# A modulated recurrence and a top-2 expert layer on one core: another first stage, and the last blocks' loads in branches

## The chip, the cores and the metric

The kernel runs on one core of a Trainium2 chip. A core has five engines with an instruction queue each: TensorE (PE in the profile, with its weight loads as PEld), VectorE (DVE), ScalarE (ACT), GpSimd (POOL) and SyncE (SP), and DMA engines that move data between the memory and the core. SP only starts DMAs here. The engines wait for one another and for DMAs through semaphores, each in the order of its own queue. The metric is the time of one execution on the device in microseconds (us). The median of three runs before is 823.8.

## The reference

The input x has 4 batches of 1024 tokens with 256 numbers each. A small product gives six rows per batch (shift, scale and gate for each of two layers). The first layer is a gated linear recurrence, the second a mixture of 8 experts of which each token uses two.

```python
mod = (_silu(L0_c) @ L0_wmod).reshape(L0_c.shape[0], 6, 1, -1)
sa, ca, ga, sb, cb, gb = (mod[:, 0], mod[:, 1], mod[:, 2], mod[:, 3], mod[:, 4], mod[:, 5])
h = _layernorm(x, axis=-1) * (1 + ca) + sa
x = x + ga * _L0_attn_ref(h, ...)
h = _layernorm(x, axis=-1) * (1 + cb) + sb
x = x + gb * _L0_ffn_ref(h, ...)
# first layer, on the rms-normalized h (256 -> 512 -> 256)
K = sigmoid(xn @ W_K)
u, g_in, g_out = split(xn @ W_ugg, 3)
u = u * sigmoid(g_in) * (1.0 - K)
outputs = scan along the tokens: s[t] = K[t-1] * s[t-1] + u[t]
y = (outputs * sigmoid(g_out)) @ W_out + residual
# second layer: softmax over 8 experts, the best two, rescaled to sum 1
output += (gelu(x @ W1[e] + b1[e]) @ W2[e] + b2[e]) * combine_w[e]
```

The two gates ga and gb have their size raised to at least 0.25 with the sign kept. All is in 32-bit floats.

## The kernel before

**Order.** The order of the work on each engine is written out by hand: instructions enter the queues as the program issues them, and no scheduler moves them. Waits are put in by the framework from what each instruction reads and writes.

**First stage.** SP loads c, then wmod in two pieces (the first 512 columns, then the other 1024), wk, the three parts of wu, x of chunk 1, wo and x of chunk 2; ACT's queue loads x of chunk 0. `sc` is c times its sigmoid; PE turns it (L251) into `scT` (4 columns) and DVE spreads batch 0 over 128 columns (`scB`). With scB, `first_rows` (L272) makes the first five modulation rows of batch 0, already spread over all partitions, in three products pm, pm1 and pm2. DVE makes `mda` (shift and 1 + scale) from pm; ACT copies pm1 and pm2 into `mdf`, between the four squares of chunk 0. With scT, `all_rows` (L286) makes the six rows for all four batches; they are finished in `other_rows` and stored to a small `rows` buffer in memory, from which later batches load their copies.

**First layer.** The 4096 tokens are 8 chunks of 512 tokens, two to a batch. For a chunk, `a_stats` and `shift` compute the statistics (a power on POOL), `a_norm` normalizes on ACT in four tiles of 128 tokens, `a_mod` applies scale and shift on DVE over the whole chunk (L365, L366), `a_square` sums squares on ACT, `a_root` and `a_scale` scale (with a power on POOL), and `a_turn` transposes on PE; ACT copies the two halves to `hT`. `project(c, hc)` runs four times per chunk: four products (pk, pgi, pu, pgo; L429) in four PSUM banks, the sigmoids on ACT, the recurrence as a scan on DVE. While chunk c is projected, the next chunk is prepared in calls between the products. `a_skip` (the residual) and `scale_out` (the gate folded into W_out) come early in a batch's first chunk. The gate row gb of a batch is loaded by SP (`load_gb`) and stored next to each token's row by ACT's queue (`store_gb`, L337).

**Second layer.** Each token's two choices go into lists per expert, and the lists are cut into blocks of 256 tokens of one expert (128 in a half block). A block j needs its list entries (`ent`, loaded by SP), its rows (two gathers by POOL, `fetch_rows`, L801) and its expert's weights (`fetch_weights`, SP, L819 to L822; 1 MB each for w1 and w2). `work` does a first product with gelu (`b_up`, L859), transposes the next block's rows (`b_turn`, L843) and a second product (`b_down`, L889); DVE adds the bias and multiplies with the weights, and POOL adds the rows to the output in memory (`add_rows`, L876). In the last blocks the rows of the last part are kept in `last_y`, with their places in `last_at`, and added at the start of the next block.

**Last blocks.** How many blocks there are depends on the data: at least 32 and at most 39. From block 28 on, `work_either` chooses between a whole and a half block (L1074); from block 32 on `rest` is a nest of branches on the number of blocks (L1105), each inside the one before. At the start of block j, `fetch(j)` starts the rows of j + 2 and the weights of j + 1, whether these blocks exist or not. A branch is taken by all five engines, each on its own copy of the number.

Of the kernel before, what the change touches and what calls it, by code (L numbers as in the profile page):

```python
# [9 lines left out]
F32 = mybir.dt.float32  # L10
I32 = mybir.dt.int32
AF = mybir.ActivationFunctionType
ALU = mybir.AluOpType
# [6 lines left out]
def tile_adaln_block(  # L20
# [33 lines left out]
    P = 128  # L54
# [191 lines left out]
    nc.scalar.activation(sc, c_sb, AF.Sigmoid)  # L246
    nc.vector.tensor_mul(sc, sc, c_sb)
    scT = setup.tile([P, KC, B], F32, tag="scT", name="scT")
    pt = ps_tr.tile([P, TB], F32, tag="tr", name="pt_c")
    for k in range(KC):  # L250
        nc.tensor.transpose(pt[:, k * B : (k + 1) * B], sc[:, ts(k, P)], ident[:B, :B])  # L251
# [1 line left out]

    scB = setup.tile([P, KC, P], F32, tag="scB", name="scB")
    nc.vector.tensor_copy(scB, scT[:, :, 0:1].broadcast_to((P, KC, P)))
    mda = deep.tile([P, 2, D], F32, tag="mda", name="mda_0")
    mdf = deep.tile([P, 3, D], F32, tag="mdf", name="mdf_0")
    with nc.allow_non_contiguous_dma(reason="a few hundred elements, once"):
        nc.scalar.dma_start(out=rms_sb, in_=rms_scale.rearrange("(k p) -> p k", p=P))
        nc.scalar.dma_start(out=split_sb, in_=split_scale.rearrange("(k p) -> p k", p=P))  # L260
# [3 lines left out]
    X[0]["stats"] = stats(X[0]["x"], "a0")  # L264
    shift(0)
    a_norm(0)

    def first_rows(i: int):
        w = min(TB, 5 * D - i * TB)
        pm = ps_mm.tile([P, TB], F32, tag="mm", name=f"pm0_{i}")  # L270
        for k in range(KC):
            nc.tensor.matmul(  # L272
                pm[:, :w],
                lhsT=scB[:, k, :],
                rhs=wmod_sb[:, k, ds(i * TB, w)],
                start=(k == 0),
                stop=(k == KC - 1),
            )
        return pm

    rows_sb = setup.tile([B, 6, D], F32, tag="rows_sb", name="rows_sb")

    def all_rows(i: int):
        pm = ps_mm.tile([P, TB], F32, tag="mm", name=f"pm_{i}")
        for k in range(KC):
            nc.tensor.matmul(  # L286
                pm[:B, :],
                lhsT=scT[:, k, :],
                rhs=wmod_sb[:, k, ts(i, TB)],
                start=(k == 0),  # L290
                stop=(k == KC - 1),
            )
        nc.scalar.copy(rows_sb[:, 2 * i : 2 * i + 2, :].rearrange("b r d -> b (r d)"), pm[:B, :])

    pm = first_rows(0)
    nc.vector.tensor_scalar_add(mda[:, 1, :], pm[:, D:], 1.0)
    nc.scalar.copy(mda[:, 0, :], pm[:, :D])
    pm1, pm2 = first_rows(1), first_rows(2)

    def other_rows():  # L300
        for j in (1, 4):
            nc.vector.tensor_scalar_add(rows_sb[:, j, :], rows_sb[:, j, :], 1.0)
        for j in (2, 5):
            clamp_gate(rows_sb[:, j, :], f"r{j}")
        nc.sync.dma_start(out=rows, in_=rows_sb)
        b1T = setup.tile([P, E, FC], F32, tag="b1T", name="b1T")
        pb = ps_tr.tile([P, TB], F32, tag="tr", name="pt_b1")
        nc.tensor.transpose(pb[:, : E * FC], b1_sb, ident[: E * FC, : E * FC])
        nc.vector.tensor_copy(b1T.rearrange("p e c -> p (e c)"), pb[:, : E * FC])
        nc.sync.dma_start(out=lists.rearrange("(p r) c -> p r c", p=P), in_=pre)  # L310
        with nc.allow_non_contiguous_dma(reason="rows of 32 bytes, once"):
            nc.sync.dma_start(out=b1d.rearrange("e p c -> p e c"), in_=b1T)


    MDA, MDF = {0: mda}, {0: mdf}

    def load_mda(b: int):
        if b < B:
# [15 lines left out]

    def store_gb(b: int):
        hx_gates.append(
            nc.scalar.dma_start(  # L337
                out=hx[ts(b, S), D:].rearrange("(n p) d -> p n d", p=P),
                in_=GB[b].unsqueeze(1).broadcast_to((P, NT, D)),
            )  # L340
        )

    def wide_row(row):
        return row.unsqueeze(1).broadcast_to((P, TPB, D))
# [10 lines left out]
    def a_stats(c_):  # L355
        X[c_]["stats"] = stats(X[c_]["x"], f"a{c_}")

    def a_mod(c_, by_tile: bool = False):
        h, md = X[c_]["h"], MDA[c_ // NB]
        if by_tile:  # L360
            for n in range(TPB):
                nc.vector.tensor_mul(h[:, n, :], h[:, n, :], md[:, 1, :])
                nc.vector.tensor_add(h[:, n, :], h[:, n, :], md[:, 0, :])
        else:
            nc.vector.tensor_mul(h, h, wide_row(md[:, 1, :]))  # L365
            nc.vector.tensor_add(h, h, wide_row(md[:, 0, :]))  # L366

    def a_square(c_, also=()):
        u = work.tile([P, TPB, D], F32, tag="u", name=f"u_{c_}", bufs=1)
        X[c_]["u"] = u  # L370
        h = X[c_]["h"]
        ss = small.tile([P, TPB], F32, tag="ss", name=f"ss_{c_}")
        X[c_]["ss"] = ss
        for n in range(TPB):
            nc.scalar.activation(
                u[:, n, :], h[:, n, :], AF.Square, accum_out=ss[:, n : n + 1]
            )
            if n < len(also):
                also[n]()

    def a_root(c_):
        ss = X[c_]["ss"]
        nc.vector.tensor_scalar(ss, ss, 1.0 / D, 1e-30, ALU.mult, ALU.max)
        nc.gpsimd.tensor_tensor(ss, ss, expo[:, 1, :], ALU.pow)

    def a_scale(c_):
        h, ss, u = X[c_]["h"], X[c_]["ss"], X[c_]["u"]
        nc.vector.tensor_scalar_add(ss, ss, RMS_EPS)
        nc.vector.reciprocal(ss, ss)
        for n in range(TPB):  # L390
            nc.vector.tensor_scalar_mul(u[:, n, :], h[:, n, :], ss[:, n : n + 1])
# [433 lines left out]
    def fetch(j: int):  # L825

        fetch_rows(j + 2)
        fetch_weights(j + 1)

    def wait_for(ins, others):  # L830
        for other in others:
            tc.add_manual_dep(
                ins.ins, other.ins.name,
                mybir.DependencyInfo(mybir.DependencyClass.Sync, mybir.DependencyReason.DATA),
                reason="all of it is there",
            )
# [46 lines left out]
    def b_down(j: int, half: bool = False, mid=None, keep: bool = False):  # L883

        g, w2, b2b, ent, hb = (BK[j][n] for n in ("g", "w2", "b2b", "ent", "hb"))
        for t in range(1 if half else HK):
            py = ps_y.tile([P, D], F32, tag="y", name=f"pye_{j}_{t}_{half}")
            for fc in range(FC):
                nc.tensor.matmul(  # L889
                    py,  # L890
                    lhsT=g[:, fc, ts(t, P)],
                    rhs=w2[:, fc, :],
                    start=(fc == 0),
                    stop=(fc == FC - 1),
                )
            kept_back = keep and t == (0 if half else HK - 1)
            if kept_back:
                yb, at = last_y, last_at
            else:
                yb = xpool.tile([P, D], F32, tag="yb", name=f"yb_{j}_{t}_{half}", bufs=3)  # L900
                at = ent[:, t, 0:1]
            nc.vector.tensor_add(yb, py, b2b)  # L902
            nc.vector.scalar_tensor_tensor(  # L903
                yb, yb, ent[:, t, 1:2].bitcast(F32), hb[t][:, D:], ALU.mult, ALU.mult
            )
            if kept_back:
                nc.vector.tensor_copy(last_at, ent[:, t, 0:1])
                continue
            if t > 0:
                nc.gpsimd.memset(between, 0.0)  # L910
            ins = add_rows(yb, at, seen(j))
            for other in BK[j]["acc"]:
                tc.declare_no_dep(ins.ins, other.ins, reason="a block's tokens are distinct")
            BK[j]["acc"].append(ins)
            if t == 0 and mid is not None:
                mid()


    a_mod(0)
    a_square(  # L920
        0,
        [
            lambda: nc.scalar.copy(mdf[:, 0:2, :].rearrange("p r d -> p (r d)"), pm1),
            lambda: nc.scalar.activation(
                mdf[:, 2, :], pm2[:, :D], AF.Identity, bias=ones[:, 0:1]
            ),
        ],
    )
    a_root(0)
    nc.vector.tensor_mul(rs_sb, rms_sb, split_sb)  # L930
    for i in range(6 * D // TB):
        all_rows(i)
    a_scale(0)
    a_turn(0)
    clamp_gate(mdf[:, 0, :], "0")
    a_stats(1)
    for c_ in range(NCH):
        nxt, prv, old = c_ + 1, c_ - 1, c_ - 2
# [12 lines left out]
        drain(6)  # L951
        if more:
            a_mod(nxt)
        a_skip(c_)
        if was:
            o_pe(prv)
            o_resid(prv)
        if placed is not None:
# [4 lines left out]
            load_mdf(b + 1)  # L963


        if part == 0:
            scale_out(b)
        if was:
            f_stats(prv)
        project(c_, 1, [lambda: a_square(nxt)] if more else [])  # L970
        if c_ == 0:
            other_rows()
        drain(6)
        if placed is not None:
            r_rank_pe(placed)
# [41 lines left out]
            a_stats(c_ + 2)  # L1017


        if was:  # L1020
            f_mod(prv)
            f_store(prv)
# [75 lines left out]
        ends_at[0:1, 1:2], min_val=sure, max_val=NJ, skip_runtime_bounds_check_because=why  # L1098
    )
    for j in range(sure_whole, sure):  # L1100
        fetch(j)
        work_either(j, j == sure - 1)

    def rest(j: int):
        with tc.If(n_blocks > j):  # L1105
            add_rows(last_y, last_at, T)
            fetch(j)
            work_either(j, True)
            if j + 1 < NJ:
                rest(j + 1)  # L1110
# [37 lines left out]
```

## Time and profile before

| what | us |
|---|---|
| median of three runs (lowest, highest) | 823.8 (823.59, 825.05) |
| the profiled execution's own time | 824.49 |
| its span, from the first to the last instruction | 822.8 |
| TensorE busy | 800.3 |
| first projection product starts | 19.78 |
| last matmul ends | 809.99 |
| last scatter to the output starts | 813.97 |

All times in the profile count from the first instruction of the profiled execution. A row of a group or of the timeline gives start, duration, engine, line and operation, written as out<-in, and in brackets the idle time before it and what ended it. In the chain of waits each piece is what the end of the execution depended on, followed backwards. A queue's own instructions (DMA starts, branches) have a q behind the engine's name. [...] each product of 256 rows deep weights (two halves of 128) shows as four matmuls.

### The profile page before, as it was taken

To read this page: it belongs to the slowest core of one execution; us is meant where nothing else is said; L and a number is where in the kernel's file an instruction comes from. 1 tells how busy PE (TensorE), PEld (TensorE's weight loads), DVE (VectorE), ACT (ScalarE), POOL (GpSimd) and SP (SyncE) were. 2 spreads that over 40 slices of the span, in tenths; PEclk is the share of its full clock that TensorE was granted. 3 is DMA by queue.
4 is the path that set the end of the run, shared out by engine and by line. 5 is a ranking of instruction groups with operands and counts; after the bars stand their busy time and mean duration, and the time that the engine had idled before them with its cause. 6 is when DMAs were issued, how large, how long until landed. Compare 5 with 4: busy or idle time off the path is not lost.

```text
span 822.8 us, 10559 instructions
## 1 busy us (share of the span) xinstructions
PE 800.3 (97%) x3447; PEld 604.8 (74%) x3447; DVE 349.3 (42%) x811; ACT 250.7 (30%) x577; POOL 300.7 (37%) x378
## 2 busy tenths in 40 slices
PE   6999999999999999999999999999999999999983
PEld 2454656564656558888888888888888888888973
DVE  4887776797788846554211112111111112111211
ACT  4434243534253243222222221312222221312221
POOL 2003010108302830788742433434342433434432
PEclk9999999999999999999999999999999999999998
DMA  9041222114101265598787677868677777867693
GB/s 305 4 113 45 81 91 72 46 51 78 45 27 33 78 187 160 146 252 206 187 258 233 180 213 209 232 199 225 192 222 200 217 217 208 231 192 199 178 329 105
DMA packets 110048, 132.57 MB, mean 161 GB/s; under 512 B 25686, under 2 KB 93978, under 8 KB 109984
## 3 DMA queue, kind: packets, MB, share of 16 engines
q1 hardware_dynamic: 86480, 101.76, 40.3%
q0 software_dynamic: 17776, 25.25, 13.7%
q10 hardware_dynamic: 5728, 4.77, 2.2%
q8 instruction: 33, 0.54, 0.3%
q14 instruction: 31, 0.25, 0.1%
HBM read 113.53 MB, written 21.75 MB: 164 GB/s over the span
## 4 chain that ended last, share of the span: by engine, by line
PE 83%; DMA 7%; DVE 4%; issue 3%; POOL 1%; ACT 1%; POOLq 0%; SPq 0%; another core or an unknown queue 0%; DVEq 0%
PE ph_False L859 24%; PE pye_False L889 23%; PE pya L466 7%; PE pk L429 6%; PE pu L429 6%; PE pgi L429 6%; PE pgo L429 6%; DMA out_dram<-yb_False,ent 3%; DMA out_dram<-last_y,last_at 2%; PE pl L540 2%; PE ptx L843 2%; DMA hb<-hx,ent 1%; PE ptf L403 1%; DMA ent<-lists 1%; PE pta L403 1%
## 5 line engine op out<-in xcount | busy, mean ns | idle before, releaser
L889 PE MATMUL pye_False<-w,g_False 128*128 128x256 f32 x992 | 219.4, 379 | 0.0
L859 PE MATMUL ph_False<-xT,w 128*128 128x256 f32 x992 | 219.2, 379 | 0.0
L859 PEld LDWEIGHTS ph_False<-xT,w 128*128 128x128 f32 x992 | 188.3, 190 | 25.5
L889 PEld LDWEIGHTS pye_False<-w,g_False 128*128 128x128 f32 x992 | 186.1, 190 | 24.0
L868 ACT ACTIVATE g_False<-ph_False,bb 128x256 f32<-128x256 f32 x248 | 104.1, 471 | 313.1 <-issue 225.3
L876 POOL DMA_INDIRECT out_dram<-yb_False,ent x46 | 73.8, 1604 | 188.6 <-DVE yb_False L903 188.6
L845 DVE COPY xT<-ptx 128x512 f32<-128x512 f32 x37 | 25.6, 691 | 197.0 <-PE ptx L843 197.0
L902 DVE TENSOR_TENSOR yb_False<-pye_False,b2b 128x256 f32<-128x256 f32 x62 | 26.3, 424 | 154.8 <-PE pye_False L889 154.8
L559 POOL DMA_INDIRECT lists<-pay,placei x64 | 68.2, 1066 | 12.5 <-issue 11.5
L801 POOL DMA_INDIRECT hb<-hx,ent x60 | 63.0, 1050 | 23.5 <-issue 16.2
L429 PE MATMUL pk<-hT,wk_sb 128*128 128x512 f32 x128 | 61.0, 599 | 0.8 <-ACT hT L405 0.8
L429 PE MATMUL pu<-hT,wu_sb 128*128 128x512 f32 x128 | 60.2, 592 | 0.0
L429 PE MATMUL pgo<-hT,wu_sb 128*128 128x512 f32 x128 | 60.1, 592 | 0.0
L429 PE MATMUL pgi<-hT,wu_sb 128*128 128x512 f32 x128 | 60.1, 592 | 0.0
L466 PE MATMUL pya<-wo,z 128*128 128x256 f32 x256 | 56.6, 379 | 0.0
L214 POOL TENSOR_TENSOR rstd_f<-rstd_f,expo 128x4 f32<-128x4 f32 x8 | 8.2, 1019 | 131.5 <-DVE rstd_f L213 131.5
L466 PEld LDWEIGHTS pya<-wo,z 128*128 128x128 f32 x256 | 48.6, 190 | 9.5 <-issue 3.3
L429 PEld LDWEIGHTS pgi<-hT,wu_sb 128*128 128x128 f32 x128 | 24.3, 190 | 30.6 <-issue 30.6
L429 PEld LDWEIGHTS pgo<-hT,wu_sb 128*128 128x128 f32 x128 | 24.3, 190 | 30.6 <-issue 26.5
L429 PEld LDWEIGHTS pu<-hT,wu_sb 128*128 128x128 f32 x128 | 23.7, 190 | 26.8 <-issue 24.4
L429 PEld LDWEIGHTS pk<-hT,wk_sb 128*128 128x128 f32 x128 | 23.1, 190 | 24.9 <-issue 20.5
L446 DVE TENSOR_TENSOR nu<-nu,pu 128x512 f32<-128x512 f32 x32 | 22.0, 686 | 45.5 <-PE pu L429 33.8
(189 smaller groups left out, 754.4 us busy)
## 6 DMA issues: line engine op xcount, KB each, us to landing
w<-in_L_ffn_W_dram SPq DMA_DIRECT2D x74, 1024.0 KB, 6.4
b2b<-in_L_ffn_b_dram SPq DMA_DIRECT2D x37, 128.0 KB, 6.7
hx<-gb ACTq DMA_DIRECT2D x4, 1024.0 KB, 7.1
out_dram<-x SPq DMA_DIRECT2D x8, 512.0 KB, 3.4
hx<-h SPq DMA_DIRECT2D x8, 512.0 KB, 3.4
x<-in_L_attn_x_dram SPq DMA_DIRECT2D x7, 512.0 KB, 7.2
wu_sb<-in_L_attn_W_ugg_dram SPq DMA_DIRECT2D x3, 512.0 KB, 5.2
mdf<-rows SPq DMA_DIRECT2D x3, 384.0 KB, 4.4
```

Source lines behind the costliest of these rows:

```text
L403: nc.tensor.transpose(pt[:, ts(t, P)], src[:, t, ts(k, P)], ident)
L429: nc.tensor.matmul(ps, lhsT=w[:, k, col : col + P], rhs=hT[:, k, :], start=(k == 0), stop=(k == KC - 1),)
L446: nc.vector.tensor_mul(nu, nu, product(wu_sb, hc * P, "u"))
L466: nc.tensor.matmul(py[:, t, :], lhsT=z[hc][:, ts(2 * q + t, P)], rhs=wo[:, hc, :], start=(hc == 0), stop=(hc == HC - 1),)
L559: ins = nc.gpsimd.indirect_dma_start(out=lists[:, :], out_offset=IndirectOffsetOnAxis(ap=place, axis=0), in_=what, in_offset=None, bounds_ ...
L801: nc.gpsimd.indirect_dma_start(out=g, out_offset=None, in_=hx[: seen(j), :], in_offset=IndirectOffsetOnAxis(ap=BK[j]["ent"][:, t, 0:1], ax ...
L845: nc.vector.tensor_copy(xT, pt)
L859: nc.tensor.matmul(ph[:, u, :], lhsT=w1[:, k, ts(fc, P)], rhs=xT[:, k, :n], start=(k == 0), stop=(k == KC - 1),)
L868: nc.scalar.activation(g[:, fc, :n], ph[:, u, :], AF.Gelu_apprx_tanh, bias=bb[:, fc : fc + 1])
L876: return nc.gpsimd.indirect_dma_start(out=out_rows[:n], out_offset=IndirectOffsetOnAxis(ap=at, axis=0), in_=yb, in_offset=None, bounds_che ...
L889: nc.tensor.matmul(py, lhsT=g[:, fc, ts(t, P)], rhs=w2[:, fc, :], start=(fc == 0), stop=(fc == FC - 1),)
L902: nc.vector.tensor_add(yb, py, b2b)
```

## The change

In the first stage `first_rows` with pm1 and pm2 is gone. Only pm is made for batch 0, later in program order; the two modulation operations take it straight from PSUM, tile by tile; `mda` is filled behind the squares, and mdf for batch 0 is loaded from the `rows` buffer like that of the other batches. `keep_busy(n)` issues n transposes of the constant identity into an unused bank, at three places. The turn of chunk 0 goes tile by tile, and DVE copies its second half to hT. `other_rows` moves up ahead of chunk 1's statistics, `a_skip` and `scale_out` of chunk 0 move back behind chunk 2's, and the gate's store goes from ACT's queue to SP's. In the last blocks `fetch_used` puts the loads that belong to blocks from 32 on into branches of their own. `last_at` is copied ahead of the last rows instead of behind them.

```diff
+    idle = ps_y.tile([P, TB], F32, tag="y", name="idle")
+    def keep_busy(n: int):
+        for _ in range(n):
+            nc.tensor.transpose(idle[:, :P], ident, ident)
+    keep_busy(14)
     pt = ps_tr.tile([P, TB], F32, tag="tr", name="pt_c")
...
     nc.vector.tensor_copy(scB, scT[:, :, 0:1].broadcast_to((P, KC, P)))
+    keep_busy(8)
...
-    pm = first_rows(0)
-    nc.vector.tensor_scalar_add(mda[:, 1, :], pm[:, D:], 1.0)
-    nc.scalar.copy(mda[:, 0, :], pm[:, :D])
-    pm1, pm2 = first_rows(1), first_rows(2)
...
-            nc.scalar.dma_start(
+            nc.sync.dma_start(
                 out=hx[ts(b, S), D:].rearrange("(n p) d -> p n d", p=P),
...
+    def fetch_used(j: int):
+        def used(i: int, step):
+            if i < sure:
+                step(i)
+            elif i < NJ:
+                with tc.If(n_blocks > i):
+                    step(i)
+        used(j + 2, fetch_rows)
+        used(j + 1, fetch_weights)
...
             if kept_back:
                 yb, at = last_y, last_at
+                nc.vector.tensor_copy(last_at, ent[:, t, 0:1])
...
-    a_mod(0)
-    a_square(
-        0,
-        [
-            lambda: nc.scalar.copy(mdf[:, 0:2, :].rearrange("p r d -> p (r d)"), pm1),
-            lambda: nc.scalar.activation(
-                mdf[:, 2, :], pm2[:, :D], AF.Identity, bias=ones[:, 0:1]
-            ),
-        ],
-    )
+    pm = ps_mm.tile([P, TB], F32, tag="mm", name="pm0")
+    for k in range(KC):
+        nc.tensor.matmul(
+            pm, lhsT=scB[:, k, :], rhs=wmod_sb[:, k, :TB], start=(k == 0), stop=(k == KC - 1)
+        )
+    h = X[0]["h"]
+    for n in range(TPB):
+        nc.vector.scalar_tensor_tensor(
+            h[:, n, :], pm[:, D:], 1.0, h[:, n, :], ALU.add, ALU.mult
+        )
+        nc.vector.tensor_add(h[:, n, :], h[:, n, :], pm[:, :D])
+    a_square(0)
+    nc.scalar.copy(mda[:, 0, :], pm[:, :D])
     a_root(0)
+    nc.vector.tensor_scalar_add(mda[:, 1, :], pm[:, D:], 1.0)
     nc.vector.tensor_mul(rs_sb, rms_sb, split_sb)
     for i in range(6 * D // TB):
         all_rows(i)
+    keep_busy(18)
     a_scale(0)
-    a_turn(0)
-    clamp_gate(mdf[:, 0, :], "0")
+    pts = [ps_tr.tile([P, TB], F32, tag="tr", name=f"pta0_{k}") for k in range(KC)]
+    for t in range(TPB):
+        for k in range(KC):
+            nc.tensor.transpose(pts[k][:, ts(t, P)], X[0]["u"][:, t, ts(k, P)], ident)
+    nc.scalar.activation(hT[:, 0, :], pts[0], AF.Copy, scale=rs_sb[:, 0:1])
+    nc.vector.tensor_scalar_mul(hT[:, 1, :], pts[1], rs_sb[:, 1:2])
+    other_rows()
+    load_mdf(0)
     a_stats(1)
...
-        a_skip(c_)
         if was:
+            a_skip(c_)
...
-        if part == 0:
+        if part == 0 and was:
             scale_out(b)
...
         if c_ == 0:
-            other_rows()
+            first_contents()
...
+        if not was:
+            a_skip(c_)
+            scale_out(b)
...
-        fetch(j)
+        fetch_used(j)
         work_either(j, j == sure - 1)
...
         with tc.If(n_blocks > j):
             add_rows(last_y, last_at, T)
-            fetch(j)
+            fetch_used(j)
             work_either(j, True)
```

More of the change, by code (lines that the diff above doesn't have):

```diff
@@ L255, in tile_adaln_block @@
     nc.vector.tensor_copy(scB, scT[:, :, 0:1].broadcast_to((P, KC, P)))
+    keep_busy(8)
     mda = deep.tile([P, 2, D], F32, tag="mda", name="mda_0")
-    mdf = deep.tile([P, 3, D], F32, tag="mdf", name="mdf_0")
     with nc.allow_non_contiguous_dma(reason="a few hundred elements, once"):
@@ L266, in tile_adaln_block @@
     a_norm(0)
[L268 to L277, printed above, removed]
-            )
-        return pm
     rows_sb = setup.tile([B, 6, D], F32, tag="rows_sb", name="rows_sb")
@@ L305, in other_rows, with first_contents @@
         nc.sync.dma_start(out=rows, in_=rows_sb)
+    def first_contents():
         b1T = setup.tile([P, E, FC], F32, tag="b1T", name="b1T")
@@ L312, in other_rows @@
             nc.sync.dma_start(out=b1d.rearrange("e p c -> p e c"), in_=b1T)
-    MDA, MDF = {0: mda}, {0: mdf}
+    MDA, MDF = {0: mda}, {}
     def load_mda(b: int):
@@ L356, in a_stats, with a_mod, a_square @@
         X[c_]["stats"] = stats(X[c_]["x"], f"a{c_}")
-    def a_mod(c_, by_tile: bool = False):
+    def a_mod(c_):
         h, md = X[c_]["h"], MDA[c_ // NB]
[L360 to L368, printed above, removed]
+        nc.vector.tensor_mul(h, h, wide_row(md[:, 1, :]))
+        nc.vector.tensor_add(h, h, wide_row(md[:, 0, :]))
+    def a_square(c_):
         u = work.tile([P, TPB, D], F32, tag="u", name=f"u_{c_}", bufs=1)
@@ L377, in a_square @@
             )
-            if n < len(also):
-                also[n]()
     def a_root(c_):
@@ L906, in b_down @@
             if kept_back:
-                nc.vector.tensor_copy(last_at, ent[:, t, 0:1])
                 continue
@@ L916, in b_down @@
                 mid()
-    a_mod(0)
-    a_square(
-        0,
-        [
-            lambda: nc.scalar.copy(mdf[:, 0:2, :].rearrange("p r d -> p (r d)"), pm1),
-            lambda: nc.scalar.activation(
-                mdf[:, 2, :], pm2[:, :D], AF.Identity, bias=ones[:, 0:1]
-            ),
-        ],
-    )
+    pm = ps_mm.tile([P, TB], F32, tag="mm", name="pm0")
[11 more added lines that the diff above has]
+    nc.scalar.copy(mda[:, 0, :], pm[:, :D])
     a_root(0)
+    nc.vector.tensor_scalar_add(mda[:, 1, :], pm[:, D:], 1.0)
     nc.vector.tensor_mul(rs_sb, rms_sb, split_sb)
@@ L932, in tile_adaln_block @@
         all_rows(i)
+    keep_busy(18)
     a_scale(0)
-    a_turn(0)
-    clamp_gate(mdf[:, 0, :], "0")
+    hT = deep.tile([P, KC, TB], F32, tag="hT", name="hT_0")
+    X[0]["hT"] = hT
+    pts = [ps_tr.tile([P, TB], F32, tag="tr", name=f"pta0_{k}") for k in range(KC)]
[6 more added lines that the diff above has]
+    load_mdf(0)
     a_stats(1)
```

## The prediction

> **What bounds the kernel now.** I read the shares first, then the windows, then the chain of waits at both ends, because a core that is busy 97% of the time has its idle time in few places.
>
> ```profile
> span 822.8 us, 10559 instructions
> PE 800.3 (97%) x3447; PEld 604.8 (74%) x3447; DVE 349.3 (42%) x811; ACT 250.7 (30%) x577; POOL 300.7 (37%) x378
> ```
>
> TensorE (PE) is idle for 22.5 us. The windows (PE busy time is the third number) say where:
>
> ```profile
> 19.80:49.20 29.40, 28.99 (x74) 12.93 (x74) 23.92 (x55) 11.51 (x30) 2.01 (x2) 1.00 0.19 39
> 49.20:776.00 726.80, 726.56 (x3132) 558.77 (x3133) 309.10 (x711) 221.00 (x495) 277.22 (x315) 1.00 0.57 159
> 776.00:810.00 34.00, 31.36 (x210) 28.10 (x208) 6.66 (x16) 9.15 (x32) 14.59 (x12) 1.00 0.90 287
> 810.00:822.80 12.80, 0.00 (x0) 0.00 (x0) 0.97 (x3) 0.00 (x0) 1.62 (x1) 0.71 0.06 7
> ```
>
> From 49 to 776 us PE loses 0.24 us: nothing that the change does to other engines there can show. What counts is when the first projection starts (19.78), a hiccup at 49.20, and what follows the last matmul (810.0). The chain of the beginning (start, duration, what):
>
> ```profile
> 1.26 4.89 DMA wmod_sb<-in_L_wmod_dram
> 6.29 3.68 PE pm L272 x4
> 10.00 0.43 DVE mda L296
> 10.53 1.24 DVE h L365
> 11.86 1.24 DVE h L366
> ...
> 13.62 0.47 ACT mdf L923
> ...
> 15.69 0.03 DVE ss L383
> ...
> 19.78 1.98 PE pk L429 x4
> ```
>
> Four matmul halves of 512 columns take 3.68 us here; the next groups of four take 1.72. The array runs at half rate until 9.80: matmul starts are 0.85 apart before it, 0.43 after. Then two whole-width operations, then squares with two copies for mdf (0.47 and 0.36) between them. The hiccup, in time order:
>
> ```profile
> 46.99 0.38 ACTq L337 DMA_DIRECT2D hx<-gb  x1
> 47.42 0.60 ACT L439 ACTIVATE kt<-pk 128x512 f32<-128x512 f32 x1 [5.68 <-PE pu L429]
> 49.20 1.55 PE L429 MATMUL pk<-hT,wk_sb 128*128 128x512 f32 x3 [0.41 <-ACT hT L405]
> ```
>
> ScalarE (ACT) stands 5.7 us before the store of the gate, because that store waits for gb (issued 44.06, landed 46.97), and the copy of hT for chunk 1 is behind it. The end, POOL's operations:
>
> ```profile
> 803.75 1.61 POOL L876 DMA_INDIRECT out_dram<-last_y,last_at  x1 [3.52 <-DMA ent<-lists]
> 805.66 1.04 POOL L801 DMA_INDIRECT hb<-hx,ent  x1 [0.30 <-issue]
> 807.01 1.00 POOL L801 DMA_INDIRECT hb<-hx,ent  x1 [0.31 <-PE pye_True L889]
> 813.97 1.62 POOL L876 DMA_INDIRECT out_dram<-last_y,last_at  x1 [5.97 <-issue]
> ```
>
> DVE has the last rows ready at 811.96, but their scatter starts at 813.97: POOL is held in the exit of the nested branches (the chain of waits comes to it from the gather of 805.66). 37 weight loads were issued, so the last block is number 35 and the gathers at 805.66 and 807.01 are for block 37, which doesn't exist. The trace's events say that POOL waits there for the scatter of 803.75 (landed 810.76) and that gather (811.06), and then raises a DMA counter until 812.72, an operation which is on the page of the branch line too:
>
> ```profile
> L1074 POOLq INC_SWDGE_SEM  x5: 1361/1448/1568, 771.8 to 805.0; - x5
> ```
>
> **The change, part by part.** *New first stage.* 14 turns of the constant now stand ahead of pt_c. The constant is ready at 1.37 (POOL's select, 1.08 + 0.29); a cold turn of 128 columns is a quarter of 0.85, 0.21 (0.233 if the warm pitch of 0.1166 in the half blocks is doubled), so they end at 1.45 + 3.0 to 3.3 = 4.4 to 4.7, and pt_c comes at about 4.6, not 3.59. Behind it on DVE wait scT, scB and then the statistics of x, which began at 4.93 (x landed at 4.90). scB's end moves from 4.46 to 5.2 to 5.6: the statistics are 0.4 to 0.7 late, I take 0.55. So the first normalized tile, 8.26 + 0.52 before, is there at about 9.4. The new product pm starts when wmod is there (6.15, unchanged; the 8 further turns end before) at 6.3 and takes 1.72 + 0.26 if the array is fast: 8.3. So h decides, not pm, with 1.1 us to spare. The modulation is 8 operations of 128x256 out of PSUM; the nearest rows (L902, L903) follow each other by 0.40 to 0.46: 3.4 to 3.7, I take 3.6, end 13.0. The last tile's square and readout take 0.51 (15.16 to 15.67 before), so the root's operation starts at 13.6 instead of 15.69: **-2.1**. Everything to pk (pow 1.02, scaling, turns, hT) follows at the same distance: pk at 17.7. On PE, pm, 12 matmul halves for all rows (12 x 0.43) and 18 turns (18 x 0.11) end at 8.0 + 5.2 + 2.0 = 15.2, before the first scaled tile (15.7). The copy of the second half of hT on DVE beside ACT's takes away the small stall of the first pk (1.98 against 1.72; half of it start-up): **-0.1**.
>
> [...] The row: half rate until 3.5 us of continuous matmuls had passed (6.29 to 9.80). [...] all turns here are transposes, and no stretch of this trace has only turns. By the row alone the array is fast by about 5 to 8 us and pm costs nothing. [...] I take the row, since real matmuls and turns use the same array[...].
>
> *Moved work.* other_rows (ten DVE operations, 37.99 to 41.11, so 3.1) goes ahead of the statistics of chunk 1: their normalization on ACT comes about 6.9 us after pk, not 4.2. PE needs the bank that ACT frees behind it (go of part 0) 12.0 after pk, and gets it at 9.5: hidden with 2.5 to spare. a_skip and scale_out (3 x 1.22) go behind the statistics of chunk 2, ahead of the last part's nu: that frees its bank at about pk + 28.6, needed at pk + 31.8. If these covers were gone, PE would wait one for one. SP issues the rows' store 20 us sooner, then mdf(0), and load 3 of x moves behind both (from 13.05 to about 24; its statistics run near 65). The gate's store is now on SP, where the next things behind it (x, hx) are wanted tens of us later, and ACT is free: the 0.41 at 49.20 and the slow start after it go, **-0.5**.
>
> *The end.* Three loads fall away: rows 36, rows 37, weights 36 (0.5 + 0.5 + 2.1 MB). None was wanted by PE, but they ran at 0.86 of all DMA engines from 802 to 810. The scatter of 803.75 took 7.0 us to land among them; the last one, alone, took 3.8 (813.97 to 817.77). After: it lands at about 807.6 to 808.5 on the old time scale, DVE needn't wait for it (810.95 becomes 810.0), the rows are ready at 811.0 and the scatter can go at 811.2. POOL now raises a counter for the skipped gather (1.45), for the half block (1.45) and at the exit (1.5): 804.5 to 808.0, then to about 810.1, and 1.25 to the scatter as before (812.72 to 813.97): 811.4. So POOL and DVE meet, and it starts at 811.4 or so instead of 813.97: **-2.5**. last_at's copy only changes sides. If the scatter still takes 7.0 to land, POOL is free at 813.6 and the part is worth 0.3.
>
> *What the branches cost.* Two more branches for each of blocks 31 to 35, one in 30, on every engine. Compare-and-branch has 0.05 us on ACT, SP, DVE and POOL and 0.18 on PE in this trace; PE's for block 35 ran at 798.7, 3.5 us ahead of the work. Hidden, except some 0.2 on SP per block while DMA is full (0.99 and 1.05 of the engines from 783 to 802). I put **+0.3**; bounds 0 and 1.5.
>
> Sum: -2.1 - 0.1 - 0.5 - 2.5 + 0.3 = -4.9 against the profiled execution's span of 822.8 (its own time is 824.5, the median of the runs 823.8; the difference lies outside the parts that change). Predicted: 823.8 - 4.9 = **818.9**.
>
> **Rivals.** (1) *The turns don't warm the array*: first stage -0.8, sum -3.6, 820.2. [...] against it nothing that this trace can show. (2) *The end stays*: the scatter lands late anyway or the three counter raises hold POOL; then -2.6, 821.2. For it: each raise is 1.4 to 1.6. (3) *Loads in line, slower*: in the built program a completion semaphore is reused after four loads in the branches, not eight; the load bb of the next block waits for w2 of this one, and w2 for b2b. On the old scale w2 of block 34 is issued at 790.1 (b2b landed 789.84), not 783.8, and needed at 798.8; that of 35 at 797.2, needed at 806.4. Rooms of 8.7 and 9.2 us, and landings in this stretch are 4.8 / 6.9 / 11.8 (least, median, most). At 11.8 each PE waits 3.1 + 2.6 = 5.7: 824.6, slower. It decides from (8.7 + 9.2 + 4.9) / 2 = 11.4 us per load. Against it: less is then in flight. (4) *A cover is gone in chunk 0*, PE waits 2 us for a bank: 820.9.
>
> **How the numbers follow.** 0.50 for the forecast (its own range 817.8 to 820.0), 0.23 for rival 1, 0.13 for rival 2, 0.05 for rival 3, 0.09 for rival 4 and lesser slips. Below 817.6 a gain would be needed that no step above holds; about 1 in 10 is left on either side of 817.6 to 821.6. A measurement of this kernel tells 0.2% (1.65 us) from no change: faster (below 822.15) takes the forecast, rival 1, nearly all of 2 and most of 4, 0.89; same 0.06; slower 0.05.
>
> **What would show it.** pk first at about 17.7; pm's four halves in 1.7 (row)[...]; no hx store on ACT and no wait at the second chunk's pk; three weight and row loads fewer; the last scatter 1.4 us or so after the last matmul instead of 4. Wrong if pk stays above 19, if PE waits in the half blocks grow beyond today's 2.6 us (the windows: 34.00 less 31.36), or if the exit still holds POOL.

## The result

The changed kernel takes 817.2 us (median of 8 runs) beside 823.7 for the kernel before: ratio 0.9926, 95% interval 0.9905 to 0.9946. Timed again beside other runs of the kernel before it took 817.6 where that one took 824.4, ratio 0.9919 (0.9900 to 0.9938). The prediction was 818.9, which is 0.9941 of 823.8: the direction and most parts held, and the gain (6.5 and 6.9 us) is 1.6 to 2.0 us larger than the sum of 4.9. The first median lies 0.4 below the range that was given (817.6 to 821.6), the second at its lower end.

The profiled execution of the changed kernel took 816.9. The first rows of its page, and its windows with the same bounds of stages as before (first projection, second chunk's first projection, late blocks, what follows the last matmul). A window's row gives its bounds and length, then busy time and count of PE, PEld, DVE, ACT and POOL, then granted clock, DMA share and GB/s:

```profile
span 815.1 us, 10691 instructions
PE 800.9 (98%) x3479; PEld 608.3 (75%) x3479; DVE 350.1 (43%) x814; ACT 249.9 (31%) x574; POOL 299.1 (37%) x374
```

```profile
17.30:46.14 28.84, 28.84 (x73) 13.14 (x74) 24.49 (x56) 11.66 (x29) 3.93 (x3) 1.00 0.45 133
46.14:770.00 723.86, 723.62 (x3120) 556.16 (x3119) 308.43 (x710) 220.67 (x493) 276.75 (x313) 1.00 0.56 157
770.00:805.30 35.30, 33.42 (x223) 30.66 (x221) 7.55 (x18) 9.64 (x34) 11.55 (x9) 1.00 0.77 234
805.30:815.10 9.80, 0.00 (x0) 0.00 (x0) 0.91 (x2) 0.00 (x0) 1.55 (x1) 0.77 0.09 11
```

TensorE is busy 0.6 us longer and idle 14.2 us instead of 22.5. The idle time shrank in three places: before the first projection, ahead of the second chunk's, and at the end. (A fourth, the half blocks, differs from one execution to the next; see below.) The chain of waits at the beginning:

```profile
1.43 3.25 PE idle L254 x14
4.68 0.32 PE pt_c L259 x2
...
5.51 0.67 DVE st_a L210 x2
6.18 1.94 PE pm L920 x4
8.12 5.24 PE pm L281 x12
13.36 2.12 PE idle L254 x18
15.48 1.05 PE pta L943 x7
16.53 0.02 issue
16.55 0.70 ACT hT L944
17.25 0.04 issue
17.30 1.98 PE pk L414 x4
```

The product pm now takes 1.94 instead of 3.68, and PE is busy almost without a pause from 1.43 to 16.5. The first projection starts at 17.30, not 19.78. The window 17.30 to 46.14 has no idle time at all: the hiccup ahead of the second chunk's projection (then 0.41) is gone. At the end, POOL's two scatters and what DVE does between them:

```profile
799.10 1.58 POOL L874 DMA_INDIRECT out_dram<-last_y,last_at  x1 [7.63 <-DVE last_y L902]
802.95 0.15 DVE L897 COPY last_at<-ent 128x1 int32<-128x1 int32 x1 [0.30 <-DMA out_dram<-last_y,last_at]
805.79 0.48 DVE L902 SCALAR_TENSOR_TENSOR last_y<-last_y,ent,hb 128x256 f32<-128x256 f32 x1
806.61 1.55 POOL L874 DMA_INDIRECT out_dram<-last_y,last_at  x1 [5.93 <-DVEq L1120]
```

No gathers stand between the two any more. The first scatter landed after 3.8 us (802.93) instead of 7.0, and the last one starts 1.32 after the last matmul (805.30) instead of 3.99.

### The profile page after: what moved, and what is told of

Its sections match the earlier page's. It is cut to its first block, busy times and chain, and to the rows that moved or that the text cites. A ratio compares the mean times of both kernels' runs of the same rounds, so it can differ in the third digit from the quotient of the medians.

```text
span 815.1 us, 10691 instructions
## 1 busy us (share of the span) xinstructions
PE 800.9 (98%) x3479; PEld 608.3 (75%) x3479; DVE 350.1 (43%) x814; ACT 249.9 (31%) x574; POOL 299.1 (37%) x374
## 4 chain that ended last, share of the span: by engine, by line
PE 94%; DMA 4%; DVE 1%; issue 0%; POOLq 0%; ACT 0%; SPq 0%; POOL 0%; DVEq 0%
PE ph_False L857 26%; PE pye_False L887 25%; PE pk L414 7%; PE pya L451 7%; PE pu L414 7%; PE pgo L414 7%; PE pgi L414 7%; DMA hb<-hx,ent 2%; PE ptx L841 2%; PE pl L525 2%; PE ptf L388 1%; PE pta L388 1%; DMA w<-in_L_ffn_W_dram 1%; PE idle L254 1%; PE pm L281 1%; DMA ent<-lists 1%
## 5 line engine op out<-in xcount | busy, mean ns | idle before, releaser
L786 POOL DMA_INDIRECT hb<-hx,ent x56 | 59.0, 1054 | 18.7 <-issue 15.9
```

The lines of the kernel that those rows point to most:

```text
L786: nc.gpsimd.indirect_dma_start(out=g, out_offset=None, in_=hx[: seen(j), :], in_offset=IndirectOffsetOnAxis(ap=BK[j]["ent"][:, t, 0:1], ax ...
```

## The experiments

**The two halves of the change.** First the stage alone (the late loads as before, `last_at` copied behind the last rows):

```diff
-        fetch_used(j)
+        fetch(j)
```

> The new first stage and the moves around it, with the last blocks' loads as before. My theory after the two profiles (first projection 2.5 us sooner, hiccup at the second chunk 0.6 gone, the rest at the end): about 3.1 us less than before, 820.6 (ratio 0.9962), and the 1.5 us that the half blocks gained is not there, nor the shorter exit. Rival: the half blocks' gain is a matter of where the transfers happen to lie and comes with any shift of the start: then 4.6 less, 819.1.

Measured: 821.4, ratio 0.9963 (0.9950 to 0.9976), 3.0 us less: the 3.1 of my theory is inside the interval, the rival's 4.6 is not. First projection at 17.28, second chunk's at 46.13 with no gap, the last scatter 5.1 after the last matmul. Then the late loads alone, on the kernel before (`fetch_used` and the early copy of `last_at` put in):

> The branches for the last blocks' loads and the early copy of last_at alone, on the first stage of before. Theory: the exit gains 2.7 to 3.0 and the half blocks 1.5, together 4.2 to 4.5 less than before, 819.4 (0.9947). Rival (the half blocks' gain belongs to no part of the change): 2.7 to 3.0 less, 820.9. If the two parts don't overlap, the two kernels' gains add up to that of the whole change.

Measured: 821.8, ratio 0.9972 (0.9962 to 0.9981), 2.3 us less; the last scatter 1.32 after the last matmul, PE's waits in the half blocks 2.6. Here my theory (4.2 to 4.5 less) fell, and the rival (2.7 to 3.0) lies inside the interval. The product of the two ratios is 0.9935, inside the interval of the whole change: within the noise the parts add up. The 1.5 us that the half blocks seemed to have gained in the first profile do not show in this time.

**The kernel before, once more,** for how much one execution differs from the next:

> The kernel before once more, for a second look at its last blocks: if the waits of TensorE in the half blocks (2.6 us in the first profile) are the same to 0.3 us, the transfers there lie the same each time and the 1.5 us that the changed kernel gained there need a cause; if they differ by a microsecond, chance is enough.

Measured: 824.0; first projection at 19.86, PE's waits in the half blocks 2.0 instead of 2.6, in other places than in the first profile. That is neither the 0.3 nor the microsecond that I had named, but all profiles together show a wider spread. From the fifth turn of rows from the end (`ptx`, near 770) to the last matmul the 14 profiled executions of this study take 36.2 to 38.0 us: 37.0 to 37.9 with the late loads as before (3 executions), 36.2 to 38.0 with all of them in branches (9; the changed kernel's own two have 36.2 and 36.4), 36.3 and 36.8 in the two runs further down that keep one kind of them. So no cost of the branches can be told from this spread, nor a gain in the half blocks.

**The turns.** All 40 taken out:

```diff
-    keep_busy(14)
...
-    keep_busy(8)
...
-    keep_busy(18)
```

> The whole change without the 40 turns of the constant. Theory that the turns raise the clock: the array is at half rate for pm (3.4 us from 6.2, ready at 9.9 instead of 8.1), the modulation starts at 9.9 instead of 9.4 but the statistics come 0.5 sooner and don't matter then; the first projection comes at 17.8 to 18.0 instead of 17.3, and the kernel is 0.5 to 0.7 slower than with them. Rival: the turns do nothing that counts, because the late scT costs what the clock gives; then within 0.2 of the whole change.

Measured: 819.1, ratio 0.9939 (0.9916 to 0.9963): by time not to be told from the whole change. By the profile the first projection starts at 17.89, 0.6 later than with them and 1.9 sooner than in the kernel before. The timeline of PE in this run:

```profile
6.33 3.55 PE L918 MATMUL pm<-wmod_sb,scB 128*128 128x512 f32 x4 [2.40 <-DMA wmod_sb<-in_L_wmod_dram]
9.81 5.31 PE L279 MATMUL pm<-wmod_sb,scT 128*4 128x512 f32 x12
16.00 1.23 PE L940 MATMUL pta<-ident,u 128*128 128x128 f32 x8 [0.88 <-DVE u L374]
17.89 1.98 PE L412 MATMUL pk<-hT,wk_sb 128*128 128x512 f32 x4 [0.67 <-ACT hT L941]
19.71 1.88 PE L412 MATMUL pgi<-hT,wu_sb 128*128 128x512 f32 x4
```

pm is slow again (3.55, its end at 9.88), and then h waits for pm: in the windows DVE is busy for 0.01 us from 9 to 10 and for 0.96 from 10 to 11. So 1.9 of the stage's 2.5 us, in this execution at least, come without the turns, from the rest of the new stage: modulation and turn by tile, and no copies for mdf between the squares. These weren't run apart. Next, only the last 18 turns taken out:

> The changed kernel without the last 18 turns, with the 14 and 8 before them. Mine (the clock, once full, outlasts a pause of 2 us): first projection at 17.3 to 17.4 and its four matmuls in 2.0. Rival (the pause before the turns of the scaled tiles sets the clock back): the turns of u and the projection run slower, first projection at 17.8 or later. Both: the first chunk's modulation is unchanged, since it lies ahead of them.

Here my expectation fell, and the rival held in part. PE's timeline (its last row is the changed kernel's pgi, for comparison), and the windows of the run without the last turns (the number ahead of the last two is the granted clock):

```profile
8.46 5.31 PE L281 MATMUL pm<-wmod_sb,scT 128*4 128x512 f32 x12
15.38 1.23 PE L942 MATMUL pta<-ident,u 128*128 128x128 f32 x8 [1.61 <-DVE u L376]
17.28 3.45 PE L414 MATMUL pk<-hT,wk_sb 128*128 128x512 f32 x4 [0.67 <-ACT hT L943]
20.57 1.88 PE L414 MATMUL pgi<-hT,wu_sb 128*128 128x512 f32 x4
19.12 1.88 PE L414 MATMUL pgi<-hT,wu_sb 128*128 128x512 f32 x4
```

```profile
13.45:16.86 3.41, 1.55 (x9) 0.81 (x8) 2.19 (x9) 1.71 (x4) 1.01 (x1) 1.00 1.06 350
16.86:20.28 3.42, 3.00 (x4) 1.45 (x5) 3.25 (x11) 0.36 (x1) 0.00 (x0) 0.50 0.76 242
20.28:23.70 3.42, 3.42 (x9) 1.51 (x9) 2.15 (x11) 1.34 (x4) 1.01 (x1) 1.00 0.07 13
```

The first projection starts at 17.28 as I thought, but after a stretch of 3.41 us in which PE was busy for 1.55 the clock is halved for the next 3.41, and pk takes 3.45 instead of 1.98. The pgi behind it starts at 20.57, not 19.12 as in the changed kernel: in this execution the missing 18 turns cost 1.45 us. Without any turns it started at 19.71, so here turns at the beginning alone were worse than none: they let the row products end early (13.8 instead of 15.1) and so open a pause of 1.6 where no turns at all leave one of 0.9. This execution took 819.5.

It is one execution, but the trace's record of the clock shows more. In all these records the stretches between two changes of the clock are whole multiples of 3.41 us (the lengths are given further down). Counted back from where it fell at the end of two runs, these are the stretches with the last matmuls and the ones behind them (two rows of the kernel before, then two of the run with rows kept, further down):

```profile
808.46:811.87 3.41, 1.52 (x8) 0.99 (x6) 0.88 (x3) 0.00 (x0) 0.00 (x0) 1.00 0.13 25
811.87:815.29 3.42, 0.00 (x0) 0.00 (x0) 0.09 (x2) 0.00 (x0) 1.32 (x1) 1.00 0.00 0
804.53:807.95 3.42, 1.39 (x7) 0.88 (x5) 0.91 (x2) 0.00 (x0) 0.65 (x1) 1.00 0.04 7
807.95:811.36 3.41, 0.00 (x0) 0.00 (x0) 0.00 (x0) 0.00 (x0) 1.62 (x1) 0.50 0.00 0
```

With 1.52 busy the full clock stayed for the next stretch (with 1.62 in the changed kernel too); with 1.39 it fell. The 1.55 of the run without the last turns fell as well, so the profile's busy time gives the bound only roughly, between 1.4 and 1.6. For the way up, 2.70 busy were not enough (late loads alone, 5.61 to 9.02), 3.00 were (16.86 to 20.28, in the table above this one). So in these rows a pause counts by how much of it falls into one stretch of 3.41, and as the stretches lie otherwise in each execution, the halving isn't shown for every one.

**The gate's store back on ACT's queue:**

```diff
-            nc.sync.dma_start(
+            nc.scalar.dma_start(
                 out=hx[ts(b, S), D:].rearrange("(n p) d -> p n d", p=P),
```

> The changed kernel with the gate's store back on ACT's queue, all else as changed. Mine (the queue move removes the hiccup): ACT stands some 5 us before the store again and the second chunk's first projection has its gap of 0.4 to 0.8 again, so it starts 29.3 to 29.8 after the first one (before: 29.4 and 29.8; changed: 28.85). Rival (the earlier store of the rows lets gb land so early that the store would not be late on any queue): gap below 0.1, distance 28.9. The first projection at 17.3 in both.

Measured: the distance of the two projections is 28.85, with no gap. My cause fell and the rival held: the move to SP isn't needed. Whether it would have been enough alone, with the rows stored late, wasn't run. ACT's timeline:

```profile
38.64 0.60 ACT L432 ACTIVATE go<-pgo 128x512 f32<-128x512 f32 x1 [2.90 <-PE pgo L414]
38.72 0.38 ACTq L329 DMA_DIRECT2D hx<-gb  x1
40.30 0.60 ACT L424 ACTIVATE kt<-pk 128x512 f32<-128x512 f32 x1 [1.06 <-PE pk L414]
```

The store waits for nothing: the rows are stored at 20.6 instead of 41.3 (`other_rows` moved up), so gb is asked for at 33.7 and landed at 37.0, 1.7 ahead of the store. Before, it was asked for at 44.1 and landed at 46.97, with ACT waiting for it.

**The end, loads one kind at a time.** First the weights of the block that doesn't exist loaded after all, then its rows and those of the one behind it:

```diff
-        used(j + 1, fetch_weights)
+        fetch_weights(j + 1)
```

> The changed kernel with the weights of the block behind the last one loaded after all, its rows not. Mine (three transfers among which the second last scatter lands, the weights the largest with 2.1 MB): that scatter takes 5 to 7 us to land again and the last scatter starts 2.5 to 4 us after the last matmul, not 1.3. Rival (it is POOL, held by the two gathers of the rows, alone): 1.3 to 1.6.

```diff
-        used(j + 2, fetch_rows)
+        fetch_rows(j + 2)
```

> The changed kernel with the rows of the two blocks behind the last one gathered after all, their weights not. Mine (landing of the second last scatter and POOL's counter raises behind it share the cost): the last scatter starts 1.3 to 3 us after the last matmul. Rival (POOL alone, held by the gathers): 3.5 to 5, as before the change; a third (weights alone): 1.3.

Measured, from the last matmul to the last scatter: 3.9 with the weights, 3.3 with the rows (3.9 to 5.1 with both, 1.3 with neither where nothing else was late). For the weights the 2.5 to 4 held, but not by the landing that I named (4.1, not 5 to 7): the scatter ahead of it took 8.4 to land, and the next rows were written late. Since that one takes 6.9 and 8.2 in two executions of the changed kernel, one execution doesn't show that the weights made it slow, and their part stays open. For the rows 3.3 is a little over my 3 and under the 3.5 of the rival, whose mechanism (POOL held by the gathers) is the one that shows. POOL in that run:

```profile
799.23 1.60 POOL L874 DMA_INDIRECT out_dram<-last_y,last_at  x1 [1.95 <-DVE last_y L902]
802.84 1.04 POOL L786 DMA_INDIRECT hb<-hx,ent  x1 [2.00 <-PE ptx L841]
804.18 1.00 POOL L786 DMA_INDIRECT hb<-hx,ent  x1 [0.31 <-issue]
809.23 1.62 POOL L874 DMA_INDIRECT out_dram<-last_y,last_at  x1 [4.05 <-issue]
```

The second gather landed at 806.31, 2.1 us after its start, and even so it held the end. One sum fits all 14 executions within 0.06 us: the last scatter starts 1.32 after the last matmul, or 2.85 to 2.92 after the landing of the last DMA that POOL had started before, whichever is later. The 2.9 hold the raise of the exit's counter (1.51 to 1.59) and 1.3 of branches and waits. In the table, the full clock's beginning is from the trace's record of the granted clock, and the last landing is that of the last gather or scatter ahead of the last scatter.

| kernel | full clock from | first projection | last matmul | last landing | last scatter |
|---|---|---|---|---|---|
| before | 9.75 | 19.78 | 809.99 | 811.06 | 813.97 |
| before, again | 10.29 | 19.86 | 809.76 | 810.78 | 813.69 |
| late loads alone | 12.43 | 20.50 | 810.36 | 807.75 | 811.67 |
| first stage alone | 6.26 | 17.28 | 806.96 | 809.19 | 812.10 |
| changed | 4.95 | 17.30 | 805.30 | 802.93 | 806.61 |
| changed, again | 4.75 | 17.24 | 805.48 | 804.45 | 807.30 |
| no turns | 9.54 | 17.89 | 807.71 | 805.31 | 809.03 |
| no last turns | 6.61 | 17.28 | 808.04 | 805.93 | 809.35 |
| gate's store on ACT | 5.30 | 17.27 | 806.70 | 803.62 | 808.01 |
| weights kept | 7.47 | 17.86 | 805.96 | 807.05 | 809.90 |
| rows kept | 5.82 | 17.28 | 805.92 | 806.31 | 809.23 |
| turns 9, 13, 14 | 5.28 | 16.75 | 806.38 | 806.05 | 808.90 |
| entries earlier | 6.42 | 17.34 | 805.34 | 802.86 | 806.68 |
| both of these | 7.46 | 17.41 | 806.32 | 803.24 | 807.66 |

**Towards a faster one.** The changed kernel again, and three versions beside it: the turns shared out as 9, 13 and 14 so that c is turned a us sooner, the list entries of the late blocks a block earlier in a fifth buffer, and both.

```diff
-    keep_busy(14)
+    keep_busy(9)
...
-    keep_busy(8)
+    keep_busy(13)
...
-    keep_busy(18)
+    keep_busy(14)
```

```diff
         used(j + 2, fetch_rows)
+        used(j + 3, fetch_entries)
```

> The changed kernel as it is, timed in five rounds. From the first measurement 817.2, ratio 0.9926 (0.9905 to 0.9946); the parts run alone multiply to 0.9935. Expected 0.992 to 0.994; the first projection at 17.3 to 17.9, by where the full clock begins (5 to 7.5 us).

> The changed kernel with the turns shared out otherwise: 9, 13 and 14 in place of 14, 8 and 18. c is turned at 3.6 instead of 4.6, so the statistics of x start at 4.95 instead of 5.43. Mine: first projection at 16.8, 0.5 sooner than the change: ratio to it 0.9994. Rival (PE, not DVE, sets it then: the rows' products and 14 turns end at about 15.0): no gain over 0.1.

> The changed kernel with the list entries of the late blocks loaded a block earlier than their rows are gathered (a fifth buffer for them), so that the gather does not wait 5 us for a small load that queues among full engines. Mine: the gather for block 35 starts 2 to 3.5 us sooner and PE's waits for rows in the half blocks shrink from 1.9 to 3.3 to under 1; 1.5 to 2 us, ratio to the kernel before 0.9905. Rival (the engines are full there, and what comes sooner takes longer to land): waits as before, 0.9926.

> The turns as 9, 13, 14 and the entries a block earlier, together. By the parts: 0.5 and 1.5 to 2 us under the change, about 815, ratio to the kernel before 0.9895 to 0.99. Rival (neither counts): 0.9926.

Measured ratios to the kernel before: 0.9919 (0.9900 to 0.9938), 0.9935 (0.9909 to 0.9960), 0.9918 (0.9902 to 0.9935), 0.9922 (0.9903 to 0.9940). None is faster than the change, and the gains of 0.5 and 1.5 to 2 us did not come. In the profiles the mechanisms show in part. With 9 turns the first projection came at 16.75, as expected; but that execution's half blocks took 37.8, and its scatter landed only at 806.05. With both, the full clock began late (7.46) and the first projection came at 17.41. With the earlier entries the gather for block 35 started at 784.80 instead of 785.93 (first profile of the change), 786.38 and 786.94 (the two beside it): 1.1 to 2.1 sooner, not 2 to 3.5. PE's waits for rows are gone; other waits of 0.7 each came in their place, among them:

```profile
781.38 3.81 PE L858 MATMUL ph_True<-xT,w 128*128 128x128 f32 x32 [0.72 <-SPq L822]
794.03 3.69 PE L888 MATMUL pye_True<-w,g_True 128*128 128x256 f32 x16 [0.74 <-ACT g_True L867]
```

The sum of the waits is then 1.5 (1.8 in the version with both), against 1.9 and 1.9 in the two profiles of the change. So sooner entries did not shorten this stretch, where the DMA engines were busy for 0.98 of the time (783 to 793). What bounds it in each execution stays open.

## Why the prediction was right

**First stage, -2.1: measured -2.5.** The two starts are 19.78 and 17.30. The step that was mis-sized is the modulation, whose first and last operation, with the one that starts the root behind it, are these:

```profile
9.38 0.42 DVE L925 SCALAR_TENSOR_TENSOR h<-pm,h 128x256 f32<-128x256 f32 x1 [0.67 <-ACT h L226]
12.21 0.42 DVE L928 TENSOR_TENSOR h<-h,pm 128x256 f32<-128x256 f32 x1
13.21 0.17 DVE L368 TENSOR_SCALAR ss<-ss 128x4 f32<-128x4 f32 x1 [0.58 <-ACT u L362]
```

Its 8 operations took 3.25 us (9.38 to 12.63), not 3.6. The normalized h was what the first one waited for, as written, not pm; the root started at 13.21 instead of 13.6, and from there to pk it is 4.09 in both kernels. The statistics came 0.50 late (5.43); 0.55 was put for it. On PE the 18 turns ended at 15.48, with the first scaled tile ready at 15.35: the half microsecond of room that was forecast between them was gone, so PE and DVE meet there.

**The row.** It was right for these turns. With turns in front the full clock begins between 4.75 and 7.47 us, in eight of ten executions before pm has started, so that only turns can have raised it; without them it begins between 9.54 and 12.43. In the trace's record of the granted clock the stretches of full clock, and that of half clock between two of them, are 1, 3, 232, 235 or 236 times 3.413 us (the full clock lasts 805.545 us, 236 times that, in the first profiles of the kernel before and of the changed one), and where they begin shifts from execution to execution. So I read my own base too narrowly: 9.75 is one draw of four without turns, and in the execution with the latest (12.43) the first projection starts at 20.50. Part of the gain that my sum lacks may lie here. At 7.47, a late draw with turns, the row products end at 14.1 and pk starts at 17.86, the most that was seen with turns.

**hT's second half on DVE, -0.1: not there.** The first pk still takes 1.98.

**The hiccup, -0.5: measured -0.57** (distance of the projections 29.42 and 28.84). The size was right, by luck in part, for the reason was not: I put it on the queue, and with the rows stored earlier the hiccup is gone on either queue. The change makes both, so only the run with the queue put back could tell.

**The end, -2.5: measured -2.7** from the last matmul to the last scatter, and 0.3 less from there to the end of the span (8.49 instead of 8.83). The steps were right: the scatter lands after 3.8, POOL and DVE meet. The table shows how closely: DVE was last in the first profile; POOL was, by 0.5 and 1.2, in two others with the same end (changed, again; turns 9, 13, 14). So the gain is 1.5 to 2.7 from one execution to another.

**Branches, +0.3: not seen.** It lies below what the half blocks vary by.

The parts by their measure, -2.5, -0.6, -2.7 and -0.3, make -6.1, where -4.9 was predicted; the two profiled spans differ by 7.7 and the medians by 6.5 and 6.9. Nearly all of the 1.6 between 6.1 and 7.7 is the half-block stretch, which took 36.2 in one profile and 37.7 in the other; with 36.2 to 38.0 among the runs, no cause is shown for it but chance. What the medians gained beyond 6.1, 0.4 and 0.8, isn't explained by a part of the change either.

**The rivals.** (1) Turns that don't warm the array: its -0.8 was my estimate from the trace before (turns of 0.21 and pm in 4 x 0.85, which puts pk at 19.0); refuted by pm's 1.94 and by the clock, full from 4.95. (2) The end stays: refuted by 1.32, though it is near enough that a late scatter brings 1 us of it back. (3) Loads in line: in the changed kernel's profile the second weights of blocks 34 and 35 landed 1.3 and 0.9 us before they were needed; that did not decide, and it wasn't tried by itself. (4) A cover gone in chunk 0: the window without idle time refutes it.

## What to carry to other kernels

Filler work on TensorE has to reach up to the work that counts: in the one execution without the last 18 turns, the clock fell just before the first projection and more time was lost than with no filler at all (pgi at 20.57 beside 19.71). Loads that nobody uses can set the end of a kernel: here, in all 14 executions, POOL's last scatter started no sooner than 2.85 us after the landing of the last DMA that POOL had started before, and in one execution the gathers alone moved it from 1.3 to 3.3 us after the last matmul. Look at several executions before a stage of 30 us is compared by one profile: the half blocks took 36.2 to 38.0 us in 14 of them.

## What was not expected of the hardware

A pause of 1.6 us (1.55 busy of 3.41) was enough to halve TensorE's clock for 3.41 us, while 1.52 busy kept it in another execution. Turns alone brought the full clock, from 4.75 us on at the earliest. Raising a counter for a skipped DMA took POOL 1.35 to 1.59 us. A small load of list entries took 5.1 us to land (780.02 to 785.14) in the changed kernel's first profile, where the profile's busy share of the DMA engines was 1.06.
